# Layer 0's linear attention in chunks of 64 tokens in place of 128

## The chip, the cores and the metric

One core of one Trainium2 chip. The metric is the device time of one launch in microseconds (us), as the median of several runs. The kernel before took 1550.02 us in the median of six runs (1547.88 to 1553.77).

## What is computed

Two transformer layers over x of shape 16 x 512 x 128 (batches, tokens, width) in fp32. Each layer normalises x and adds an attention and a feed-forward part to it. Layer 0 has a linear attention with 16 heads of 8, and a mixture of 8 experts (top 2) with a shared expert. Layer 1 has a softmax attention in chunks of 64 queries with a gate on each head's sum, and a channel mix. The change touches layer 0's attention alone:

```python
def step(carry, qkv):                      # over the tokens; q, k after rope and elu(x) + 1
    K_sum, KV = carry
    q_t, k_t, v_t = qkv
    K_sum = K_sum + k_t
    KV = KV + k_t[..., :, None] * v_t[..., None, :]
    num = jnp.einsum('bhd,bhde->bhe', q_t, KV)
    den = jnp.maximum(jnp.einsum('bhd,bhd->bh', q_t, K_sum), EPS)
    return ((K_sum, KV), num / den[..., None])
```

Nothing forces a step for each token: within a chunk of tokens the kernel takes scores q k^T, masks them causally and multiplies by v; all earlier chunks come in as one product of q with the running state, the sum of k v^T over them. A column of ones beside v gives the denominator.

## The kernel before

**Four chains of work.** The 16 batches go in four groups of four. For each group there are four Python generators: `dispatch` (normalise, route, and scatter the rows to their experts' slots by an indirect DMA), `slot_tiles` (the experts on 39 slots of 128 rows at the most), `layer0` (linear attention and shared expert, `first_layer` per batch) and `layer1` (`head`, `body`, `tail` per batch). Every `yield` of a generator ends a step. A loop at the end of `two_layers` gives each chain a start and a time per step, from `PACE`, `LAYER_STEPS` (steps per batch) and `LAYER_US`, and always advances the chain that is due first. That settles the rank of each operation.

**A planner.** No instruction is issued there. `Program.call` records each operation with an estimated cost, what it reads and writes, and `Program.run` simulates the five engines on these costs and emits, engine by engine, the operation of the lowest rank that is ready and whose buffers are free. So the order on each engine is the planner's, and its costs only shape that order. Operations in a `with program.unit()` are emitted together. Scatters and fetches by indirect DMA on POOL (`send`, line 1202, and `fetch`, line 1221) are kept `SPACE` ns apart on the planner's clock, and each is made to wait for the PE operation that had passed by then. Since all operations are emitted from one helper, nearly all have line 323 in the profile; line 328 is the same helper where a full matmul is emitted as four of 32 output columns each (`strips`), which the planner does when the matmul before it was not of the full form, since TensorE then needn't change its tiling.

**Layer 0's attention, per batch.** `linear_operands` makes q, k and v for four tiles of 128 tokens, applies rope and elu + 1, copies v into `vpads` (strips of 32 columns: 16 of v, two of ones, the rest belongs to the neighbour) and `vstrips`, and then the running states: for t = 0, 1, 2 a matmul of k^T with v of tile t is added into one bank of PSUM, and after each VectorE (DVE) copies the sum so far, masked by `blocks`, to `states[t]`. It transposes q and k (`qT`, `kT`), and makes four copies of `qT` with all but one of four heads' rows zeroed (`q0m`). `linear_attention` then goes through the four tiles: `scores(t)` is a unit of eight matmuls with 32 rows each (row group j of `kT` against two copies of q, 256 columns, the four j into four banks), and DVE multiplies the 4 x 512 scores by the causal mask into two `am`; `weigh(t)` is a unit on one bank with 8 matmuls of the state with q (128 rows, 32 output columns, 128 tokens; none for t = 0) and 16 of the strips of v with `am`; ScalarE (ACT) copies the result. Every second tile `finish` transposes, divides by the denominators and writes `o0n`. The first two batches run side by side, the second on buffers that layer 1 doesn't need yet (`LENT`). PSUM has eight banks, handed out by the planner, in ones or pairs.

Of the kernel before, what the change touches and what calls it, by code (L numbers as in the profile page):

```python
# [29 lines left out]
F32 = mybir.dt.float32  # L30
# [3 lines left out]
ALU = mybir.AluOpType  # L34
AX = mybir.AxisListType

P = 128
# [17 lines left out]
def slot_count(gt):  # L55
# [13 lines left out]
HALVES = 2 * NT  # L69

VPAD = (H - 1) * (PAIR + 2) + 32

# [15 lines left out]
    ("ident", P), ("cos", NT * 4), ("sin", NT * 4), ("blocks", 8 * (PAIR + 2)), ("pick", 4),  # L88
    ("causal", P), ("rank", E), ("upper", P), ("ones", P), ("tile", SLOT_TILES),
    ("aug_q", 2 * HALVES), ("aug_k", 4 * HALVES), ("own", 2), ("parity", 4),  # L90
# [16 lines left out]

LAYER_STEPS = (16, 40)

# [144 lines left out]
class Op:  # L254


    def __init__(self, engine, emit, cost, later, index):
        self.engine, self.emit, self.cost, self.later, self.index = engine, emit, cost, later, index
        self.needs, self.bases, self.wrote, self.then = set(), set(), set(), []
        self.missing, self.ready, self.result, self.done = 0, 0.0, None, False  # L260

        self.spaced = False

        self.form, self.strips, self.narrow = None, None, False

# [11 lines left out]

TURN = {(32, 128): 208, (128, 32): 138, (128, 128): 148}

SPACE = 1900  # L280

PACE = (
    (0.1, 0.4, 0.26, 0.8, 0.0, 0.8, 0.0, 1.23),
    (0.3, 0.4, 0.2, 0.8, -0.09, 1.0, 0.22, 1.0),
    (0.0, 0.58, 0.27, 0.76, 0.18, 1.0, 0.0, 1.0),
)


class Program:
# [21 lines left out]
    def call(self, name, api, method, args, kw):  # L311
# [18 lines left out]
        if name == "PE":  # L330
            later = 60.0
            form = (args[1].shape[0], o.shape[0])
            if method == "transpose":
                cost = 112.0
            elif args[1].shape[0] == 32:
                cost = max(0.425 * n, 56.0)
            elif o.shape[0] == 32:
                cost = max(0.425 * n, 56.0)
            else:
                cost = max(1.68 * n, 224.0)  # L340
# [16 lines left out]
        if name == "PE":  # L357
            (self.unit_of[0] if self.unit_of else op).form = form
            op.strips = strips if method == "matmul" and form == (P, P) else None
# [46 lines left out]
    def run(self):  # L406
# [20 lines left out]
        while emitted < len(self.ops):  # L427
# [27 lines left out]
            if op.spaced:  # L455
                self.spaced_to = start + SPACE
                while len(self.passed) > 1 and self.passed[1][0] <= start:
                    self.passed.pop(0)
                op.paced = self.passed[0][1] if self.passed else None
            end = start + op.cost  # L460
            if name == "PE":
                if self.form != (P, P) and all(part.strips for part in op.parts or [op]):
                    op.form, op.narrow = (P, 32), True
                if op.form != self.form:
                    end += TURN.get(op.form, 148)
                    self.form = op.form
            if name == "PE":
# [135 lines left out]
def two_layers(ctx: ExitStack, tc: tile.TileContext, x, small, const, w_fc, w_proj, out):  # L603
# [144 lines left out]
    states = []  # L748
    for i in range(NT - 1):
        st = fixed.tile([P, 8, 32], F32, tag=f"state{i}", name=f"state{i}")  # L750
        G.memset(st, 0.0)
        states.append(st)
# [156 lines left out]
    def tokens_to_heads(o, name, tag):  # L909
# [10 lines left out]
    OWN = {  # L920
        "vpad": 0, "qr": ("qr", 1), "T": ("q0T", "k0T", 1), "q0m": ("q0m", 2), "am": ("am", 2),
        "oTs": "oTs0", "o": "o0n", "oT": "oT_a0", "xs": ("xs", 1),
    }
    LENT = {
        "vpad": 2, "qr": ("ka", 2), "T": ("qa", "qa", 2), "q0m": ("probs", 4), "am": ("ka", 2),
        "oTs": "oTs1", "o": "o1n", "oT": "oT_a1", "xs": ("rr", 2),
    }
    OWN["vstrips"], OWN["states"] = vstrips, states

    def lent_layer():  # L930

        a = p3.tile([P, 1024], F32, tag="probs", name="vstrips_lent", bufs=4)
        LENT["vstrips"] = a[:, 0 : NT * 8 * (PAIR + 2)].rearrange(
            "p (t s e) -> p t s e", t=NT, e=PAIR + 2
        )
        G.memset(a, 1.0)
        a = p3.tile([P, 1024], F32, tag="probs", name="states_lent", bufs=4)
        LENT["states"] = [
            a[:, i * 256 : (i + 1) * 256].rearrange("p (s e) -> p s e", e=32) for i in range(NT - 1)
        ]  # L940
        G.memset(a, 0.0)

    def linear_operands(xnT, b, home):
# [50 lines left out]

        pst = one(f"state_{b}")
        for t in range(NT - 1):
            M.matmul(
                pst[:, 0 : 8 * (PAIR + 2)], qr[:, t, D : 2 * D],
                vs[:, t, :, :].rearrange("p s e -> p (s e)"),
                start=(t == 0), stop=(t == NT - 2), skip_group_check=True,  # L1000
            )
            V.tensor_tensor(
                states[t][:, :, 0 : PAIR + 2],
                pst[:, 0 : 8 * (PAIR + 2)].rearrange("p (s e) -> p s e", e=PAIR + 2), blocks,
                ALU.mult,
            )
        yield
# [3 lines left out]
        for s, (tag, n) in enumerate(((q_tag, "q0T"), (k_tag, "k0T"))):  # L1011
# [7 lines left out]
            both.append(oT)  # L1019
        qT, kT = both  # L1020
        qms = []
        for u in range(2):
            tag, bufs = home["q0m"]
            qm = (p3 if tag == "probs" else p2).tile(
                [P, 2, T], F32, tag=tag, name=f"q0m_{b}_{u}", bufs=bufs
            )
            for o in range(2):
                r = 2 * u + o
                S.activation(qm[:, o, :], qT, AF.Copy, scale=c_("pick")[:, r : r + 1])
            qms.append(qm)  # L1030
        yield
        return qT, kT, qms

    def linear_attention(operands, b, home):
# [3 lines left out]

        def scores(t):

            scs = [big(f"sc0_{b}_{t}_{pr}") for pr in range(2)]
            cols = slice(t * P, (t + 1) * P)
            with program.unit():
                for u in range(2):
                    for j in range(4):
                        rows = slice(32 * j, 32 * j + 32)
                        M.matmul(
                            scs[j // 2][:, j % 2, 2 * u * P : 2 * (u + 1) * P].rearrange(
                                "p (o q) -> p o q", o=2
                            ),  # L1050
                            kT[rows, cols], qms[u][rows, :, cols], start=True, stop=True,
                        )
            ams = []
            for pr, sc in enumerate(scs):
                tag, bufs = home["am"]
                am = p2.tile([P, 2, 512], F32, tag=tag, name=f"am_{b}_{t}_{pr}", bufs=bufs)
                V.tensor_tensor(
                    am.rearrange("p j (t q) -> p j t q", q=P),
                    sc.rearrange("p j (t q) -> p j t q", q=P),
                    causal.unsqueeze(1).unsqueeze(1).to_broadcast([P, 2, NT, P]), ALU.mult,  # L1060
                )
                ams.append(am)
            return ams

        def weigh(t, ams, oT):

            po = one(f"o0_{b}_{t}")

            with program.unit():
                for u in range(2):  # L1070
                    for j in range(4):
                        o = po[32 * j : 32 * j + 32, u * P : (u + 1) * P]
                        if t:
                            M.matmul(
                                o, states[t - 1][:, 4 * u + j, :], qT[:, t * P : (t + 1) * P],
                                start=u == 0, stop=False, skip_group_check=True,
                            )
                    for o_ in range(2):
                        c = (2 * u + o_) * P
                        for j in range(4):  # L1080
                            M.matmul(
                                po[32 * j : 32 * j + 32, u * P : (u + 1) * P],
                                strip(vp, t, 8 * u + 2 * j + o_), ams[j // 2][:, j % 2, c : c + P],
                                start=t == 0 and u == 0 and o_ == 0, stop=(o_ == 1),
                                skip_group_check=True,
                            )
            S.copy(oT[:, (t % 2) * 2 * P : (t % 2 + 1) * 2 * P], po[:, 0 : 2 * P])

# [15 lines left out]

        for t in range(NT):
            if t % 2 == 0:
                oT = p2.tile([P, T], F32, tag=home["oTs"], name=f"oTs0_{b}_{t // 2}")
            ams = scores(t)
            yield
            weigh(t, ams, oT)  # L1110
            yield
            if t % 2:
                finish(oT, t // 2)
                yield
        return tokens_to_heads(o, f"a0_{b}", home["oT"])
# [82 lines left out]
    def send(rows, slot, row, clear, sent):  # L1198
# [14 lines left out]
        i.bases.add(rows.base)  # L1213
        i.spaced = True
        after(i, [clear])
        sent.append(i)

    def fetch(o, results, slot):
# [6 lines left out]
        )  # L1225
        i.spaced = True

# [514 lines left out]
def _constants():  # L1742
# [6 lines left out]
    i = np.arange(P)  # L1749
    c["causal"] = (i[None, :] >= i[:, None]).astype(f)  # L1750
    e = np.arange(PAIR + 2)
# [84 lines left out]
```

## Time and profile before

| | |
|---|---|
| median of six runs | 1550.02 us (1547.88 to 1553.77) |
| the profiled execution | 1542.83 us, span in the profile 1541.1 us |
| mean granted clock of TensorE | 0.985 |
| instructions | 53614, of them 23070 matmul and 23070 weight-load records on TensorE |
| am, the mask on the scores (DVE) | 128 x 1219 ns, 151.0 us busy |
| states (DVE) | 48 x 303 ns, 14.5 us busy |
| matmul records of the scores, of the states with q, of v with am | 1024, 768, 2048 |

In the profile PE is TensorE's matmuls and PEld its weight loads, DVE VectorE, ACT ScalarE, POOL GpSimd. Groups are named by what they write and read: `banks<-q0m,k0T` are the scores, `banks<-am,vpad` and `banks<-q0T,state` the two parts of weigh, `banks<-vstrips,qr` the states' matmuls; `banks<-qa,ka` and `banks<-ka,qa` are layer 1's scores, of which `maxima` takes maxima and `ex` the exponential. A form such as 32\*128 stands for the rows and output columns of TensorE that a matmul uses. A matmul of fp32 is recorded twice. Records of matmuls that run side by side overlap, and their ends are modelled, so the starts are what can be relied on.

### The profile page before, as it was taken

How to read it: one execution, taken by the hardware profiler on the slowest of the kernel's cores; microseconds unless marked ns; L12 is line 12 of the kernel's file. 1: busy time of each engine (PE TensorE's matmuls, PEld its weight loads, DVE VectorE, ACT ScalarE, POOL GpSimd, SP SyncE). 2: the span in 40 equal slices, each digit the busy share in tenths (PEclk: the TensorE clock that was granted, in tenths of full speed). 3: DMA queues.
4: the chain of work that ended last, by engine and by line, in shares of the span. 5: the costliest groups of instructions: out<-in, count | busy, mean ns of one | idle time of the engine just before them, and what ended most of it. 6: DMA issues, size and time to landing. Idle time of an engine off the chain costs nothing.

```text
span 1541.1 us, 53614 instructions
## 1 busy us (share of the span) xinstructions
PE 1409.4 (91%) x23070; PEld 927.0 (60%) x23070; DVE 1067.0 (69%) x2289; ACT 864.1 (56%) x1369; POOL 390.8 (25%) x425
## 2 busy tenths in 40 slices
PE   4788989899999999999999999999999989887876
PEld 2577877666666657666666666665766545533433
DVE  7874432787877776687684868586858896865673
ACT  3335565565665655656656656755665545455434
POOL 3540142432036241215300240200001512442310
PEclk9899999999999999999999999999999999999998
DMA  6247777655254545243432434322411100000000
GB/s 195 91 151 206 214 237 206 184 164 156 75 161 138 155 142 149 74 136 118 132 93 61 126 115 128 109 85 65 126 47 46 43 21 20 17 15 8 8 1 14
DMA packets 150237, 163.08 MB, mean 106 GB/s; under 512 B 12912, under 2 KB 97648, under 8 KB 150000
## 3 DMA queue, kind: packets, MB, share of 16 engines
q1 hardware_dynamic: 141808, 142.86, 31.2%
q0 software_dynamic: 8192, 16.79, 3.4%
q8 instruction: 181, 2.97, 0.8%
q14 instruction: 56, 0.46, 0.1%
HBM read 118.71 MB, written 40.89 MB: 104 GB/s over the span
## 4 chain that ended last, share of the span: by engine, by line
PE 77%; DVE 11%; ACT 7%; issue 3%; DMA 1%; SPq 0%; POOL 0%; DVEq 0%; ACTq 0%
PE banks L323 56%; PE banks L328 21%; DVE maxima L323 5%; ACT ex L323 3%; ACT hg L323 2%; DVE am L323 1%; DVE by_cos L323 1%; ACT q0m L323 1%; DMA back<-results,pl_slot 1%; DVE by_sin L323 0%; ACT vpad L323 0%; ACT h L323 0%; DMA raw_wqkv<-in_small 0%; ACT vstrips L323 0%; DVE gf_z L323 0%
## 5 line engine op out<-in xcount | busy, mean ns | idle before, releaser
L323 DVE TENSOR_REDUCE maxima<-banks 128x2 f32<-128x768 f32 (+2 forms) x448 | 385.7, 914 | 75.6 <-PE banks L323 73.9
L323 ACT ACTIVATE ex<-banks 128x1024 f32<-128x1024 f32 x320 | 311.4, 1021 | 133.0 <-PE banks L323 127.8
L323 DVE TENSOR_TENSOR am<-banks,const_sb 128x1024 f32<-128x1024 f32 x128 | 151.0, 1219 | 108.8 <-PE banks L323 100.5
L323 PE MATMUL banks<-ka,qa 32*128 32x512 f32 (+2 forms) x1792 | 184.9, 505 | 29.5 <-ACT ex L323 18.6
L323 PE MATMUL banks<-qa,ka 32*128 32x512 f32 (+3 forms) x2048 | 192.5, 462 | 18.9 <-DVE maxima L323 11.7
L1221 POOL DMA_INDIRECT back<-results,pl_slot x128 | 127.3, 995 | 290.1 <-PE banks L323 192.9
L1202 POOL DMA_INDIRECT rows<-xn,pl_slot x128 | 127.1, 993 | 290.1 <-DVE pl_slot L323 172.9
L323 PE MATMUL banks<-ex,vpad 128*32 128x512 f32 (+3 forms) x2048 | 174.3, 443 | 2.2 <-issue 1.0
L323 PEld LDWEIGHTS banks<-qa,ka 32*128 32x128 f32 x2048 | 94.7, 185 | 94.6 <-DVE maxima L323 24.3
L323 ACT ACTIVATE hg<-banks 128x512 f32<-128x512 f32 x156 | 93.2, 598 | 99.7 <-PE banks L328 77.7
L323 PEld LDWEIGHTS banks<-ka,qa 32*128 32x128 f32 x1792 | 80.2, 185 | 93.5 <-ACT ex L323 28.7
L328 PE MATMUL banks<-xgT,wf 128*32 128x128 f32 x3296 | 109.2, 274 | 3.7 <-ACT ex L323 1.4
L323 PEld LDWEIGHTS banks<-ex,vpad 128*32 128x32 f32 x2048 | 53.3, 109 | 93.2 <-issue 63.5
L328 PE MATMUL banks<-wp,hg 128*32 128x128 f32 x3200 | 100.0, 276 | 9.6 <-ACT hg L323 4.8
L328 PEld LDWEIGHTS banks<-xgT,wf 128*32 128x32 f32 x3296 | 89.2, 110 | 29.7 <-issue 9.0
L328 PEld LDWEIGHTS banks<-wp,hg 128*32 128x32 f32 x3200 | 88.1, 111 | 28.0 <-ACT hg L323 9.5
L323 ACT COPY oTs<-banks 128x256 f32<-128x256 f32 (+1 forms) x96 | 42.8, 446 | 88.0 <-PE banks L323 84.6
L323 ACT ACTIVATE hg<-hg 128x1024 f32<-128x1024 f32 x80 | 82.9, 1037 | 2.5
L323 PE MATMUL banks<-am,vpad 128*32 128x128 f32 x2048 | 78.2, 273 | 2.6 <-DVE am L323 2.1
L323 PE MATMUL banks<-q0m,k0T 32*128 32x256 f32 x1024 | 73.3, 399 | 2.2 <-DVE am L323 0.9
L323 ACT COPY yg<-banks 128x256 f32<-128x256 f32 x80 | 29.4, 367 | 68.6 <-PE banks L328 51.6
L323 PEld LDWEIGHTS banks<-am,vpad 128*32 128x32 f32 x2048 | 58.0, 110 | 11.0 <-DVE am L323 3.1
(224 smaller groups left out, 2224.2 us busy)
## 6 DMA issues: line engine op xcount, KB each, us to landing
wf<-in_w_fc SPq DMA_DIRECT2D x156, 256.0 KB
wp<-in_w_proj SPq DMA_DIRECT2D x156, 256.0 KB
rows<-zeros SPq DMA_DIRECT2D x4, 2496.0 KB
results<-yg SPq DMA_DIRECT2D x76, 128.0 KB
xg<-rows SPq DMA_DIRECT2D x36, 256.0 KB
x_in<-in_x SPq DMA_DIRECT2D x16, 256.0 KB
x<-x SPq DMA_DIRECT2D x16, 256.0 KB
out<-rr SPq DMA_DIRECT2D x16, 256.0 KB
```

The source lines that it names most:

```text
L323: return getattr(api, method)(*map(made, args), **{k: made(a) for k, a in kw.items()})
L328: yield api.matmul(to[at : at + 32], weights[:, at : at + 32], *rest, **kw)
L1202: i = nc.gpsimd.indirect_dma_start(out=rows.made()[:, :], out_offset=bass.IndirectOffsetOnAxis(ap=slot.made(), axis=0), in_=row.made(), in ...
L1221: "POOL", lambda: nc.gpsimd.indirect_dma_start(out=o.made(), out_offset=None, in_=results.made()[:, :], in_offset=bass.IndirectOffsetOnAxi ...
```

## The change

A chunk is now 64 tokens (`CH`), eight in a batch (`CHUNKS`). Scores and weigh go over pairs of tiles, `tp`, in place of single tiles. A chunk's keys are rows of one half of the partitions: the scores of the chunk c = 0 of a tile go to partitions 0 to 63, those of c = 1 to 64 to 127, so the two bank pairs that held one tile's scores hold two tiles', and one causal mask of 64 columns serves both. Seven states are needed in place of three: seven matmuls of 64 rows in one unit, into three banks; DVE masks the first six in one instruction and the seventh in another, and adds them up in place with six additions. Weigh takes a pair of banks, one for each c; the states' matmuls have 32 rows and 32 columns now (row group j and strip j), those of v with `am` 64 rows and 32 columns. The four copies of q are one tile for the batches that use their own buffers. The planner's costs and turns get the new forms, `LAYER_STEPS`, `PACE` and the spacing of indirect DMAs other values. Beside that, the weight loads and DMAs are the same.

```diff
-LAYER_STEPS = (16, 40)
+LAYER_STEPS = (12, 40)
...
-SPACE = 1900
+SPACE = 1500
+SPACE_FIRST = 1500
 PACE = (
-    (0.1, 0.4, 0.26, 0.8, 0.0, 0.8, 0.0, 1.23),
-    (0.3, 0.4, 0.2, 0.8, -0.09, 1.0, 0.22, 1.0),
-    (0.0, 0.58, 0.27, 0.76, 0.18, 1.0, 0.0, 1.0),
+    (0.1, 0.4, 0.31, 0.8, 0.0, 0.8, 0.01, 1.28),
+    (0.3, 0.41, 0.12, 0.8, -0.26, 1.0, 0.25, 1.0),
+    (-0.27, 0.45, 0.41, 0.67, 0.05, 1.0, 0.21, 0.54),
 )
...
-        pst = one(f"state_{b}")
-        for t in range(NT - 1):
-            M.matmul(
-                pst[:, 0 : 8 * (PAIR + 2)], qr[:, t, D : 2 * D],
-                vs[:, t, :, :].rearrange("p s e -> p (s e)"),
-                start=(t == 0), stop=(t == NT - 2), skip_group_check=True,
-            )
-            V.tensor_tensor(
-                states[t][:, :, 0 : PAIR + 2],
-                pst[:, 0 : 8 * (PAIR + 2)].rearrange("p (s e) -> p s e", e=PAIR + 2), blocks,
-                ALU.mult,
-            )
+        n = 8 * (PAIR + 2)
+        pst, last = big(f"state_{b}"), one(f"state_last_{b}")
+        with program.unit():
+            for i in range(CHUNKS - 1):
+                t, c = i // 2, i % 2
+                rows = slice(c * CH, (c + 1) * CH)
+                M.matmul(
+                    pst[:, c, t * n : (t + 1) * n] if i < CHUNKS - 2 else last[:, 0:n],
+                    qr[rows, t, D : 2 * D], vs[rows, t, :, :].rearrange("p s e -> p (s e)"),
+                    start=True, stop=True, skip_group_check=True,
+                )
+        V.tensor_tensor(
+            states[0][:, :, 0:n].rearrange("p (t c) e -> p c t e", c=2),
+            pst[:, :, 0 : 3 * n].rearrange("p c (t e) -> p c t e", t=3),
+            c_("blocks").unsqueeze(1).unsqueeze(1).to_broadcast([P, 2, 3, n]), ALU.mult,
+        )
+        V.tensor_tensor(states[1][:, 0, 0:n], last[:, 0:n], c_("blocks"), ALU.mult)
+        for i in range(1, CHUNKS - 1):
+            upto = state_of(states, i)[:, 0:n]
+            V.tensor_tensor(upto, upto, state_of(states, i - 1)[:, 0:n], ALU.add)
...
+        def scores(tp):
+            scs = [big(f"sc0_{b}_{tp}_{pr}") for pr in range(2)]
             with program.unit():
+                for r, n, qm in qms:                      # own buffers: one r, n = 4
+                    for t, c, half, cols in parts(tp):    # two tiles, two chunks
+                        at = (t % 2) * 4 * CH + r * CH
+                        for j in range(4):
+                            rows = slice(32 * j, 32 * j + 32)
+                            M.matmul(
+                                scs[j // 2][half, j % 2, at : at + n * CH].rearrange(
+                                    "p (o q) -> p o q", q=CH
+                                ),
+                                kT[rows, cols], qm[rows, :, cols], start=True, stop=True,
+                            )
...
+        def weigh(tp, ams, oT):
+            po, begun = big(f"o0_{b}_{tp}"), set()
...
             with program.unit():
+                for t, c, _, cols in parts(tp):
+                    for u in range(2):
                         for j in range(4):
+                            if 2 * t + c:
+                                o, kw = to(t, c, u, j)    # strip j of bank c, 64 columns
+                                at = (4 * u + j) * (PAIR + 2)
+                                rows = slice(32 * j, 32 * j + 32)
+                                M.matmul(
+                                    o, state_of(states, 2 * t + c - 1)[rows, at : at + 32],
+                                    qT[rows, cols], stop=False, **kw,
+                                )
+                for t in (2 * tp, 2 * tp + 1):
+                    for u in range(2):
+                        for o_ in range(2):
+                            for j in range(4):
+                                for c in range(2):
+                                    half = slice(c * CH, (c + 1) * CH)
+                                    o, kw = to(t, c, u, j)
+                                    at = (t % 2) * 4 * CH + (2 * u + o_) * CH
+                                    M.matmul(
+                                        o, strip(vp, t, 8 * u + 2 * j + o_)[half, :],
+                                        ams[j // 2][half, j % 2, at : at + CH],
+                                        stop=(o_ == 1), **kw,
+                                    )
...
-        for t in range(NT):
...
+        for tp in range(NT // 2):
+            oT = p2.tile([P, T], F32, tag=home["oTs"], name=f"oTs0_{b}_{tp}")
+            ams = scores(tp)
+            yield
+            weigh(tp, ams, oT)
+            yield
+            finish(oT, tp)
+            yield
```

## Prediction

> **What bounds the kernel now.** I read the page first: its busy line for TensorE (PE), and the chain that ended last.
>
> ```profile
> span 1541.1 us, 53614 instructions
> ...
> PE 1409.4 (91%) x23070; PEld 927.0 (60%) x23070; DVE 1067.0 (69%) x2289; ACT 864.1 (56%) x1369; POOL 390.8 (25%) x425
> ...
> PE 77%; DVE 11%; ACT 7%; issue 3%; DMA 1%; SPq 0%; POOL 0%; DVEq 0%; ACTq 0%
> ```
>
> PE carries 77% of the chain, DVE 11%. But a share is an average, so I read next the windows of 100 us (columns: length, then busy time of PE, PEld, DVE, ACT, POOL).
>
> ```profile
> 0.00:100.00 100.00, 69.56 (x760) 50.05 (x761) 78.39 (x246) 34.21 (x72) 46.67 (x68) 0.91 0.42 129
> ...
> 400.00:500.00 100.00, 99.52 (x1764) 68.95 (x1766) 79.42 (x197) 62.33 (x102) 35.31 (x38) 1.00 0.43 128
> ...
> 1400.00:1541.10 141.10, 105.05 (x1184) 50.77 (x1176) 76.23 (x152) 65.09 (x84) 28.08 (x20) 0.92 0.03 9
> ```
>
> Three stages. The first 100 us leave PE 30 us idle and DVE is the fullest. From 300 to 1200 PE idles only some 20 of 900 us: there the end moves by what PE saves. The last 241 us (84.94 of 100 us busy, then 105.05 of 141.10) are layer 1 nearly alone, with 51 us of PE idle. The windows of the tile q0m place layer 0's scores: 176 of 1024 matmul records before 115.6 us and none after 1298. So 2.75 of 16 batches run in the first stage and 13.25 where PE binds or nearly.
>
> The durations of overlapping matmuls mean little, so I price by the timeline of PE, from the start of one group to the start of the next (start, length, engine, line, operands, count). Every fp32 matmul is two records: the 16 matmuls of a weigh unit on am stand as 32.
>
> ```profile
> 624.23 0.44 PE L328 MATMUL banks<-small_sb,xnT 128*32 128x8 f32 x32
> 624.51 1.08 PE L328 MATMUL banks<-xgT,wf 128*32 128x128 f32 x32
> ...
> 711.09 1.15 PE L323 MATMUL banks<-q0m,k0T 32*128 32x256 f32 x16
> 712.16 1.08 PE L328 MATMUL banks<-xgT,wf 128*32 128x128 f32 x32
> ...
> 716.04 0.43 PE L323 MATMUL banks<-q0T,state 128*32 128x128 f32 x8
> 716.29 0.62 PE L323 MATMUL banks<-am,vpad 128*32 128x128 f32 x16
> 716.72 0.40 PE L323 MATMUL banks<-q0T,state 128*32 128x128 f32 x8
> 716.94 0.62 PE L323 MATMUL banks<-am,vpad 128*32 128x128 f32 x16
> 717.49 0.66 PE L323 MATMUL banks<-const_sb,o1n 128*128 128x128 f32 x4
> ...
> 749.64 1.06 PE L328 MATMUL banks<-wpj_s,h 128*32 128x128 f32 x32
> 750.52 0.40 PE L328 MATMUL banks<-small_sb,oT_a 128*32 128x128 f32 x8
> 751.61 0.43 PE L328 MATMUL banks<-vstrips,qr 128*32 128x144 f32 x8
> 751.97 1.14 PE L323 MATMUL banks<-ka,qa 32*128 32x512 f32 x8
> ```
>
> A scores unit takes 712.16 - 711.09 = 1.07 us, a weigh unit with state 717.49 - 716.04 = 1.45 (without, at t = 0, 507.66 - 506.65 = 1.01), a state matmul 0.36. Sixteen matmuls of 128 columns on four column tiles, with the same form after them, take 750.52 - 749.64 = 0.88 us, 55 ns each; the 1.01 holds a change of form of 0.13. At 8 columns they take 624.51 - 624.23 = 0.28 us, 17.5 ns each: the floor this trace shows for one fp32 matmul with its weight load.
>
> **The change part by part**, per batch, PE first. Before: 4 x 1.07 + 1.01 + 3 x 1.45 + 3 x 0.36 = 4.28 + 5.36 + 1.08 = 10.72 us.
>
> *Scores.* Two units in place of four, each of 16 matmuls of 256 columns on eight tiles (four row groups by two halves of the output). If the halves run side by side, each tile has two matmuls, as each row group has now: 2 x 1.07 = 2.14. If only four tiles run at a time, 2 x (1.72 + 0.21) = 3.86, the 0.21 being what 1.07 holds over 4 x 256 columns at the 55 ns rate (0.86). No row has eight tiles. I take 2.14: four row groups together (q0m) and four column tiles with different moving data together (wpj_s) both have rows. [...]
>
> *Weigh, states.* 24 matmuls of 128 columns become 56 of 64 (seven chunks, two units, four strips), on the four diagonal tiles. Bounds per matmul: 17.5 ns (the 8-column row) and 55 (nothing gained from halving): 0.98 to 3.08 us. I take half of 55, 27.5, since 128 columns are far over the floor: 1.54.
>
> *Weigh, own chunk.* 64 matmuls of 128 columns become 128 of 64, with 64 rows each, on eight tiles. If eight overlap, the floor of 17.5 ns binds: 2.24 us; if four, 27.5: 3.52; by a straight line between the 8- and the 128-column rows, 35: 4.48. I take 22, midway between the first two: 2.82. Each of the two units now enters two forms, so changes stay at four: 0.52. Weigh: 1.54 + 2.82 + 0.52 = 4.88 against 5.36.
>
> *States.* Seven matmuls of 64 rows and 144 columns, in one unit. Full-array rows go one at a time at 224 ns per 128 columns (xgT,wf 128x128, cadence 112 a record), 252 for 144: 1.76 alone, or four deep in two row halves 1.01, with 0.15 of form change 1.16 to 1.91. I take 1.16, as row groups do overlap in q0m's row. The three rounds in which DVE had to read one bank before PE went on are gone; the waits view has 1.3 us for them in all, so nothing.
>
> After: 2.14 + 4.88 + 1.16 = 8.18, so PE gives back 2.54 us a batch, 40.6 in all.
>
> *DVE.* The mask on am falls from 128 to 64 instructions of 1219 ns: -78.0 us. The states' 48 of 303 ns (-14.5) become, per batch, one of 864 elements (between 690 ns at 512 and 1219 at 1024: 1.05), one of 0.30 and six adds of 144 elements (224 ns at 64, 291 at 128: 0.30), 3.15 x 16 = +50.4. Net -42 us. In the PE-bound stage that is worth nothing: DVE is at 75 to 80%. Behind the adds on DVE's queue stand layer 1's reductions of maxima, for which PE waited 21.3 us in all; a run of eight is 2 us longer than what stood there, but twice a batch two am of 2.4 us are gone from the same queue. The first weigh waits for the adds; transposes, four q0m on ACT (722 ns each) and the first am lie before it and cover them. Without that cover it would be 3 us a batch on one chain with three others to fill PE.
>
> *ACT*: 64 copies of 375 ns become 32 of 586, -5 us, off the path. *Banks*: scores hold four banks twice a batch, not four times; weigh takes two for half as many units; the states take three at once. Nothing either way.
>
> *POOL's spacing* falls from 1900 to 1500 in the planner's clock. The first 32 scatters run from 47.0 to 105.5 us, 1.83 each; 32 x 0.4 is up to 12.8 us earlier for the first slot tiles, which wait for all of them. From 100 to 140 PE idles 8.6 us, but the DMA share is 0.7 to 0.9 until 260. Bounds -9 to +5 (scatters that crowd the weights' loads); I take 0. *PACE* and LAYER_STEPS change only the order: the idle in the first and last stages, 30 + 51 us, may move by some 10 either way; I take 0.
>
> The sum: 13.25 batches x 2.54 = 33.7 us come off where PE binds. In the first stage 2.75 batches x 2.6 us of DVE = 7; half of it, 3.5, since scatters and DMA run beside. What is late next: with less of layer 0 to fill in, PE's waits on ex (24.4 us in all) and maxima (21.3) grow; a tenth of the gain, 3.5. Net -34. The profiled execution took 1542.8 us (its span 1541.1 and 1.7 around it) and would take 1509; the median of the six runs, 1550.0, lies 7.2 above it, so **1516 us**.
>
> **The rivals.** *Half of it comes back as waiting*: layer 1 alone keeps PE at 79% (190 of 241 us), 97% with fillers. If the smaller layer 0 lets one more batch of layer 1 (60 us) run alone, 60 x 0.18 = 11 us, and with worse order at the start some 17: 1533. For it: the last stage; against it: mid-run a batch of layer 1 takes 86 us, not 60, so PE is what holds it.
>
> *Better*: own-chunk matmuls at the 17.5 ns floor (0.58 a batch, 9 us) and the scatters' 9 us: 1498. For it: the idle from 100 to 140.
>
> *The tiles don't overlap (it does not do what it says)*: scores 3.86, weigh 1.54 + 3.52 + 0.52 = 5.58, states 1.91: 11.35, +0.63 x 13.25 = +8, less 3 at the start: 1555.
>
> *The other side: the states' diagonal tiles take turns.* The 56 matmuls have four row groups that write four strips of the same bank at once; in every row of the trace four row groups (q0m, qa, ka) write four banks. One at a time, a matmul of 64 columns costs half of 224 ns, 112, so 6.27 in place of 1.54: +4.73 x 13.25 = +63, and 1516 + 63 = 1579. It decides from a price of 73 ns each on, where the 34 us are gone (2.54 a batch over 56 is 45 ns above 27.5). Against it: the strips are different partitions, and column tiles of one bank do overlap in wpj_s's row. [...]
>
> **How the numbers follow.** Forecast 0.62 (1502 to 1532, from the prices of 17.5 to 35 ns and the order); half comes back 0.13; better 0.08; no overlap 0.11; turns 0.06. Faster: 0.62 + 0.13 + 0.08, less 0.02 for their upper ends, 0.81; no overlap straddles zero, 0.04 of it within 0.2%; slower 0.15. (0.2%, 3 us, is about what a measurement of this kernel can tell from no change.) The range leaves out the turns and part of the better case and takes in no overlap: 1495 to 1556.
>
> **What would show it.** The scores' form has 64 output columns, and 32 records start to start take about 1.1 us, not 1.9. A weigh unit of two tiles takes about 2.4 us, of it 0.7 to 0.9 for the states; over 4 us means turns. DVE falls to about 1025 us, PE to about 1370, and PE stays at 97% or more from 300 to 1200. If PE's busy time falls by 35 us or more and the span by less than 20, waiting has taken the place; if the span falls by over 50, the start or the order gave it.

## The result

The changed kernel takes 1558.8 us in the median of 20 runs (1550.51 to 1568.76), the kernel before 1550.18 (45 runs): ratio 1.0054, 95% interval 1.0041 to 1.0066. It is 0.5% slower; 1516 us was predicted. The profiled execution took 1564.1 us.

The profile's page after, in three lines: the span, the engines' busy time, and the DMA queue that the page marks as instruction (packets, MB, share).

```profile
span 1562.3 us, 57575 instructions
...
PE 1401.3 (90%) x25080; PEld 917.1 (59%) x25080; DVE 1029.2 (66%) x2305; ACT 856.1 (55%) x1337; POOL 389.4 (25%) x424
...
q8 instruction: 196, 3.21, 0.9%
```

DVE fell by 38 us, as forecast. PE fell by 8, not by 40, though it has more matmul records (25080 against 23070). The mean granted clock is 0.966 (0.985 before). Two windows that answer to those shown of before:

```profile
0.00:100.00 100.00, 60.40 (x1106) 40.89 (x1107) 67.62 (x229) 29.66 (x60) 42.90 (x62) 0.85 0.41 124
400.00:500.00 100.00, 96.31 (x2052) 66.52 (x2052) 76.57 (x207) 58.87 (x96) 33.37 (x36) 0.98 0.44 131
```

PE is idler at the start (60 of 100 us in place of 70, clock 0.85 in place of 0.91) and in the middle too (96.3 in place of 99.5). What it waits for is in the waits view of PE (releaser: us in total, times, longest); the first and the last line are of a kind that summed to 5.2 us before.

```profile
PE banks L331 <- issue: 31.5, 25, 3.3
PE banks L331 <- ACT ex L331: 27.4, 43, 1.2
PE banks L331 <- DVE maxima L331: 21.1, 30, 1.4
...
PE banks L336 <- issue: 4.1, 2, 2.2
```

The two lines of that kind before:

```profile
PE banks L328 <- issue: 4.2, 4, 2.2
PE banks L323 <- issue: 1.0, 1, 1.0
```

"Issue" is time for which the profile shows no semaphore. It grew by 30 us; ex and maxima hardly moved (24.4 and 21.3 before). Thirteen of the 27 waits, 20.3 us, fall before layer 1's first `ex`, which starts at 338 us (at 313 before). Where they happen is in PE's timeline:

```profile
657.04 0.87 PE L331 MATMUL banks<-q0T,state 32*32 32x64 f32 x48
657.85 1.45 PE L331 MATMUL banks<-am,vpad 64*32 64x64 f32 x124
661.49 0.30 PE L331 MATMUL banks<-am,vpad 64*32 64x64 f32 x4 [2.19 <-issue]
661.72 1.08 PE L336 MATMUL banks<-xgT,wf 128*32 128x128 f32 x32
...
730.89 0.87 PE L331 MATMUL banks<-q0T,state 32*32 32x64 f32 x48
731.70 1.48 PE L331 MATMUL banks<-am,vpad 64*32 64x64 f32 x128
733.11 0.66 PE L331 MATMUL banks<-const_sb,oTs 128*128 128x128 f32 x4
```

The same unit, twice. At 731.70 the own-chunk group of 64 matmuls takes 733.11 - 731.70 = 1.41 us to the next group. At 657.85 PE stops after 124 of 128 records, in the middle of a unit in which nothing is waited for, and the group takes 3.87. Of the 32 own-chunk groups ten take 1.41 us; the others take 1.76 to 4.82, and all together 79.7: 34.6 us more than 32 x 1.41. Of these, 28.5 lie inside the groups; the other 6 are mostly two waits behind a group, one on issue (2.24 us) and one on a DMA (3.34).

Each matmul of fp32 is two matmul and two weight-load records, four instructions (in bursts, below, 400 matmuls are 800 and 800 records). That makes 2 x 25080 / 196 = 256 instructions for each packet of q8, and 3.21 MB / 196 = 16 KB a packet. So the first theory, FETCH in the later expectations: PE uses up its instructions faster than they come. The trace's records of q8 bear it out in place: each of the 27 times that PE goes on after a wait on issue lies 2.3 to 2.9 us after a packet of q8 began, though a packet begins only every 8 us in the mean. And of TensorE's instructions ahead of each of the 27, in order of start, 193 or 194 are left over from full blocks of 256. The rivals: FORM (tiles of 64 and 32 rows overlap badly or read as idle to the clock) and ORDER (the new `PACE` and spacing are a worse order). The first expectations have ORDER against "code", which is FETCH and FORM in one.

### The profile page after: what moved, and what is told of

It is laid out like the page before. It is cut to its first block, busy times and chain, and to the rows that moved or that the text cites. A ratio compares the mean times of both kernels' runs of the same rounds, so it can differ in the third digit from the quotient of the medians.

```text
span 1562.3 us, 57575 instructions
## 1 busy us (share of the span) xinstructions
PE 1401.3 (90%) x25080; PEld 917.1 (59%) x25080; DVE 1029.2 (66%) x2305; ACT 856.1 (55%) x1337; POOL 389.4 (25%) x424
## 3 DMA queue, kind: packets, MB, share of 16 engines
q8 instruction: 196, 3.21, 0.9%
## 4 chain that ended last, share of the span: by engine, by line
PE 42%; DVE 7%; ACT 5%; issue 2%; DMA 1%; POOL 0%; DVEq 0%; ACTq 0%; POOLq 0%
PE banks L331 31%; PE banks L336 11%; DVE maxima L331 4%; ACT ex L331 4%; DMA back<-results,pl_slot 0%; DVE rr L331 0%; DVE by_cos L331 0%; DMA out<-rr 0%; DMA x<-x 0%; DVE am L331 0%; DVE by_sin L331 0%; DVE gf_z L331 0%; ACT q0m L331 0%; DVE state L331 0%; POOL xn L331 0%
## 5 line engine op out<-in xcount | busy, mean ns | idle before, releaser
L331 PE MATMUL banks<-ka,qa 32*128 32x512 f32 (+2 forms) x1792 | 194.2, 519 | 25.9 <-ACT ex L331 18.2
L331 PE MATMUL banks<-ex,vpad 128*32 128x512 f32 (+3 forms) x2048 | 178.7, 451 | 3.1 <-DVE maxima L331 1.8
L331 DVE TENSOR_TENSOR am<-banks,const_sb 128x1024 f32<-128x1024 f32 x64 | 75.5, 1219 | 47.5 <-PE banks L331 47.3
L331 ACT COPY oTs<-banks 128x512 f32<-128x512 f32 x64 | 37.5, 585 | 110.5 <-PE banks L331 110.3
L336 PE MATMUL banks<-wp,hg 128*32 128x128 f32 x2592 | 81.6, 278 | 7.7 <-DMA results<-yg 3.3
L331 POOL TENSOR_TENSOR rr<-rr,x 128x512 f32<-128x512 f32 x16 | 20.5, 1279 | 269.3 <-DVE rr L331 269.2
L336 PEld LDWEIGHTS banks<-wp,hg 128*32 128x32 f32 x2592 | 72.2, 112 | 19.8 <-issue 10.5
L331 PE MATMUL banks<-wp,hg 128*128 128x128 f32 x600 | 74.2, 276 | 0.9 <-ACT hg L331 0.8
L331 PEld LDWEIGHTS banks<-wp,hg 128*128 128x128 f32 x600 | 70.6, 192 | 6.3 <-ACT hg L331 3.8
L331 PE MATMUL banks<-am,vpad 64*32 64x64 f32 x4096 | 54.7, 225 | 21.5 <-issue 21.3
```

The costliest lines, as they stand in the source:

```text
L331: return getattr(api, method)(*map(made, args), **{k: made(a) for k, a in kw.items()})
L336: yield api.matmul(to[at : at + 32], weights[:, at : at + 32], *rest, **kw)
```

## The experiments

Ratios are to the kernel before, measured beside each run. "Issue" is the sum of PE's waits on it and "clock" the mean granted clock, both in the profiled execution.

| run | ratio (95% interval) | median, us | issue, us | clock |
|---|---|---|---|---|
| before | 1 | 1550.2 | 5.2 | 0.985 |
| after | 1.0054 (1.0041, 1.0066) | 1558.8 | 35.6 | 0.966 |
| code_old_order | 1.0302 (1.0280, 1.0323) | 1598.4 | 42.7 | 0.960 |
| before_new_order | 1.0035 (1.0018, 1.0052) | 1559.2 | 6.4 | 0.972 |
| old_pace | 1.0291 (1.0274, 1.0309) | 1596.5 | 37.7 | 0.961 |
| old_space | 1.0034 (1.0015, 1.0052) | 1558.0 | 35.6 | 0.971 |
| wide128 | 0.9835 (0.9818, 0.9852) | 1523.4 | 4.4 | 0.975 |
| wide64 | 0.9774 (0.9759, 0.9789) | 1515.4 | 9.7 | 0.970 |
| before_split | 1.0214 (1.0201, 1.0227) | 1582.4 | 12.4 | 0.977 |
| per_tile | 1.0104 (1.0084, 1.0125) | 1564.0 | 34.8 | 0.975 |
| heads_in_halves | 0.9839 (0.9808, 0.9870) | 1522.8 | 13.6 | 0.980 |
| before_split_same_order | 1.0131 (1.0101, 1.0161) | 1569.4 | 13.9 | 0.982 |
| wide64_old_pace | 0.9988 (0.9968, 1.0008) | 1549.1 | 8.5 | 0.961 |

### Is it the order? (code_old_order, before_new_order, old_pace, old_space)

The new code with the old `PACE` and spacing; the old code with the new `PACE` and a spacing of 1500; the new code with one of the two old at a time.

```diff
-PACE = ((0.1, 0.4, 0.31, 0.8, 0.0, 0.8, 0.01, 1.28), ...)    # old_pace, code_old_order
+PACE = ((0.1, 0.4, 0.26, 0.8, 0.0, 0.8, 0.0, 1.23), ...)
-SPACE = 1500                                                 # old_space, code_old_order
+SPACE = 1900
```

> The changed attention with PACE and both spacings of the kernel before (1900); LAYER_STEPS stays at 12, since a batch has 12 steps now. Theory order: the code gives back the 1.38 us a batch that the timeline of after shows on PE (10.72 before; 2.10 + 6.06 + 1.18 after), some 18 us where PE binds, and the new PACE and spacing lose 25 by starting layer 1 late; then this run takes about 1532 us, 0.988 of before, and the first ex starts at 305 to 313 us as before. Theory code: the new forms themselves cost it (weigh units with 14 ns a record, and a clock halved 109 us in all in place of 48); then it takes 1553 to 1562 as after does, and the granted clock is 0.966 to 0.974 again.

> The kernel before with PACE of after and a spacing of 1500. Theory order: 25 us slower than before, 1575 us (1.016), with the first ex some 25 us late. Theory code: within 0.3% of before, and a granted clock of 0.985.

> After with PACE of before; the spacings stay at 1500. Theory order with PACE as its cause: as in the run of the changed code with the old PACE and spacing, about 1532 us. With the spacing as its cause: 1555 to 1560. Theory code: 1553 to 1562.

> After with both spacings at 1900 and its own PACE. Theory order with PACE as its cause: 1555 to 1560 us, as after. With the spacing as its cause (scatters that crowd the loads of weights): about 1535. Theory code: 1553 to 1562.

The spacing is worth nothing (1.0034 against 1.0054, intervals that overlap). `PACE` is worth much, but the other way: with the old one the new code takes 1596.5 us, 38 more, outside the ranges of both theories. On the old code the new `PACE` and spacing cost 0.35%. So the loss isn't the new order; the issue waits are there in either.

### Fewer instructions for the same part (wide128, wide64)

The own-chunk part goes out as 32 matmuls of 128 columns, on all 128 rows (wide128) or on 64 (wide64). Both leave out separations that the result needs (their expectations say which), so they price the instructions and replace nothing. The order on every engine stays.

```diff
-for u in range(2):
-    for o_ in range(2):
-        for j in range(4):
-            for c in range(2):
-                M.matmul(o, strip(vp, t, 8 * u + 2 * j + o_)[half, :], ams[j // 2][half, j % 2, at : at + CH], ...)
+for u in range(2):
+    for j in range(4):
+        for c in range(2):
+            M.matmul(                                # wide128: without [half]
+                po[32 * j : 32 * j + 32, c, 2 * (t % 2) * CH : 2 * (t % 2) * CH + 2 * CH],
+                strip(vp, t, 8 * u + 2 * j)[half, :], ams[j // 2][half, j % 2, at : at + 2 * CH], ...)
```

> The changed kernel, but the own-chunk part of a weigh unit is issued as 32 matmuls of 128 columns on all 128 rows in place of 64 matmuls of 64 columns on 64 rows: half the PE instructions, as many columns times rows or more. (It leaves out the separation of the two chunks and of two heads of a pair: their sums are added. Order on every engine as in the changed kernel.) By the rows, 32 such matmuls take 32 x 55 ns = 1.76 us, 0.35 to 0.5 us a unit MORE than the 1.27 to 1.41 us that an unstalled own-chunk group takes: 32 units, +11 to +16 us of array work. Theory FETCH (PE runs out of instructions because the small matmuls use up 256 instructions in under 2 us): PE's waits on 'issue' fall from 35.6 us to under 12, halvings of the clock become fewer, mean clock 0.975 or more, and in spite of more array work the time falls: 1535 to 1552, ratio 0.990 to 1.001. Theory FORM (the small tiles themselves overlap badly or read as idle to the clock): no help is needed from fewer instructions; array work is added, 1565 to 1575. Theory ORDER (the new order of the engines' work is worse): as the changed kernel, 1555 to 1565, with fewer issue waits but as much idle.

> The changed kernel, but the own-chunk part is issued as 32 matmuls of 128 columns and 64 rows (form 64*32) in place of 64 of 64 columns: half the instructions in the same form of tile. (It leaves out the separation of two heads of a pair. Order as in the changed kernel.) If eight tiles overlap, 32 x 27.5 ns = 0.88 us a unit against 1.41; if only four, 1.76. Theory FETCH: 'issue' waits of PE under 12 us (35.6 in the changed kernel), own-chunk groups of 64 records 0.9 to 1.3 us and none over 2, time 1520 to 1540, ratio 0.980 to 0.993. Theory FORM: issue waits fall less than half, clock stays near 0.966, time 1548 to 1562. Theory ORDER: 1550 to 1562, fewer issue waits but the gain turned into idle on ex or banks.

wide128 does more array work, 1.95 us a group in most places where 1.41 would do:

```profile
558.61 2.02 PE L331 MATMUL banks<-am,vpad 128*32 128x128 f32 x64
560.56 1.14 PE L331 MATMUL banks<-qa,ka 32*128 32x512 f32 x8
```

Yet it is 35 us faster than the changed kernel. It has half the own-chunk instructions, but also another form and more columns in a matmul; wide64 keeps the form 64\*32, and heads_in_halves, below, the 64 columns. wide64 takes 1515.4 us. Both are faster than the ranges given for FETCH. The waits on issue of wide64:

```profile
PE banks L336 <- issue: 5.9, 4, 2.7
PE banks L331 <- issue: 3.8, 5, 1.3
```

And its timeline at the place that stalled above (the same groups in the same order):

```profile
628.70 0.87 PE L331 MATMUL banks<-q0T,state 32*32 32x64 f32 x48
629.51 1.16 PE L331 MATMUL banks<-am,vpad 64*32 64x128 f32 x64
630.59 1.08 PE L336 MATMUL banks<-xgT,wf 128*32 128x128 f32 x32
```

1.08 us in place of 3.87, in the form 64*32, next to 32*32: FORM falls. Of the 43 us between the changed kernel and wide64, 32 x (1.41 - 1.09) = 10 are array time. The other 33 went with the instructions: PE's waits on issue fell by 25.9 us, and what the own-chunk groups take over their array time by 27.2 (34.6 to 7.4). The two overlap, and the rest of the 33 wasn't traced; the clock can hold 8 of it at most by estimate, half of the difference between the 108 us for which it was at half in the changed kernel and the 92 in wide64.

### More instructions in the kernel before (before_split, before_split_same_order)

Every weigh matmul of 128 columns becomes two of 64.

```diff
-M.matmul(po[32 * j : 32 * j + 32, u * P : (u + 1) * P], strip(...), ams[j // 2][:, j % 2, c : c + P], ...)
+for q in (0, 64):
+    M.matmul(po[32 * j : 32 * j + 32, u * P + q : u * P + q + 64], strip(...),
+             ams[j // 2][:, j % 2, c + q : c + q + 64], ...)
```

> The kernel before, but every matmul of a weigh unit on 128 columns is two on 64 columns: the same sums, form, and order on every engine; 16 to 24 matmuls of a unit become 32 to 48, so 128 to 192 instructions where there were 64 to 96. Array time is the same if a matmul of 64 columns takes half of 55 ns. Theory FETCH: the before kernel's 5.2 us of 'issue' waits rise to 12 to 30, clock falls below 0.98, time +8 to +30 us, ratio 1.005 to 1.020; in this kernel other dense groups on the same instructions stand beside. Theory FORM or ORDER: forms and order are unchanged, so within 0.3%: ratio 0.998 to 1.003.

> before_split again, with the planner told the old price of a weigh unit, so that the order on all five engines is that of the kernel before, instruction for instruction but for the doubled matmuls (in before_split the planner had the price 3% lower, and the order was another). Theory FETCH: of the 33 us that before_split lost, 15 to 30 stay: array time of 12 us more (the groups' starts in before_split: own chunk 65.7 to 74.8 us, states 21.1 to 23.8) plus stalls: ratio 1.009 to 1.020, issue waits over 10 us. Rival (the 33 us were the other order): only the array's 5 to 12 us stay, ratio 1.002 to 1.008, issue waits 5 us as in the kernel before.

Of before_split's 2.1% a part was order: the planner had been given a slightly other price. With the order of the kernel before, 1.3% stay, 20 us (16 to 25). Its waits on issue:

```profile
PE banks L328 <- issue: 9.5, 11, 2.0
PE banks L323 <- issue: 4.4, 4, 2.3
```

These are 8.7 us more than before; the groups on `am` and on the states take 10.7 us more from start to start (65.7 to 74.0 and 21.1 to 23.5), a part of which is waits on issue within them. So twice as many matmuls cost time in the old code as well, some 9 of the 20 us as waits on issue.

### Units of half the size (per_tile)

```diff
-weigh(tp, ams, oT)
+weigh(2 * tp, ams, oT)
+yield
+weigh(2 * tp + 1, ams, oT)
```

(`LAYER_STEPS` rises from 12 to 14 with it.)

> The changed kernel, but weigh is one unit for each tile of 128 tokens (40 to 48 matmuls, 160 to 192 instructions) with its own pair of banks, in place of one unit for two tiles (88 to 96 matmuls, 352 to 384 instructions), so that layer 1's matmuls, with more array time per instruction, can be put between. 16 * 2 more copies of 256 columns on ACT, two more changes of form a batch (+0.3 us each), the planner's order is another. Theory FETCH: 'issue' waits of PE fall from 35.6 to under 15 us, clock 0.975 or more, time 1525 to 1548, ratio 0.983 to 0.998. Theory FORM: 1560 to 1575 (more changes of form, same tiles). Theory ORDER: anything from 1540 to 1600 and issue waits don't matter to it.

A miss: the issue waits stay at 34.8 us. One place in the timeline:

```profile
1086.13 0.43 PE L331 MATMUL banks<-q0T,state 32*32 32x64 f32 x16
1086.49 0.86 PE L331 MATMUL banks<-am,vpad 64*32 64x64 f32 x64
1087.28 0.66 PE L331 MATMUL banks<-const_sb,xg 128*128 128x128 f32 x4
1087.87 0.65 PE L331 MATMUL banks<-q0T,state 32*32 32x64 f32 x32
1088.44 0.84 PE L331 MATMUL banks<-am,vpad 64*32 64x64 f32 x63
1091.51 0.24 PE L331 MATMUL banks<-am,vpad 64*32 64x64 f32 x1 [2.22 <-issue]
```

Here the planner puts the two halves 1.7 us apart, with 0.6 us of other work between, so the same 352 instructions go out in some 3 us at PE's own pace. From the first half's own-chunk group to the second's it is 1.4 us at the least and 3.4 in the median of the 32 units; in 26 of them it is less than the 5.3 us in which 352 instructions come by the next experiment. Split in two, the units saved nothing here (34.8 us of issue waits against 35.6), as their parts stayed together.

### The supply by itself (bursts)

```diff
+for k, (rows, n) in enumerate(((128, 128), (128, 96), (128, 64), (64, 64), (128, 8))):
+    for m in range(400):
+        M.matmul(pp[32 * j : 32 * j + 32, c, 0:n], probe[half, 0, 0:32], probe[half, 0, 128 : 128 + n], ...)
```

> The kernel before, with five bursts of 400 matmuls (1600 PE instructions) after all of its work, each after 12 us or more without PE work: 128 columns, 96, 64, then 64 columns with 64 rows on eight tiles, then 8 columns; all else 128 rows, four column tiles. The total time is of no interest. Theory FETCH: without a limit they would take 400 x 55 = 22 us, 41 ns = 16.5, 27.5 ns = 11, 20 ns = 8, 17.5 ns = 7 us. If PE's instructions come in blocks of 256 (64 matmuls) and a block takes some 2 us to come, the first bursts run at their own pace, and from 64 columns on each settles at the same pace, about 2 us or more for 64 matmuls (31 ns or more each), with gaps at every 64th: the last three bursts all take 12 us or more. Rival (no limit on the stream): the last three take 11, 8 and 7 us with no gap.

PE's timeline of the second, third and fourth burst (96 columns, 64, and 64 with 64 rows):

```profile
1585.25 10.73 PE L323 MATMUL banks<-probe 128*32 128x96 f32 x427 [8.36 <-DVE probe L323]
1596.61 2.84 PE L323 MATMUL banks<-probe 128*32 128x96 f32 x128 [0.63 <-issue]
1600.37 2.84 PE L323 MATMUL banks<-probe 128*32 128x96 f32 x128 [0.91 <-issue]
...
1615.17 5.66 PE L323 MATMUL banks<-probe 128*32 128x64 f32 x267 [8.38 <-DVE probe L323]
1622.29 1.99 PE L323 MATMUL banks<-probe 128*32 128x64 f32 x128 [1.46 <-issue]
1625.76 1.99 PE L323 MATMUL banks<-probe 128*32 128x64 f32 x128 [1.48 <-issue]
1629.78 1.99 PE L323 MATMUL banks<-probe 128*32 128x64 f32 x128 [2.03 <-issue]
...
1646.51 3.38 PE L323 MATMUL banks<-probe 64*32 64x64 f32 x235 [8.44 <-DVE probe L323]
1651.47 1.47 PE L323 MATMUL banks<-probe 64*32 64x64 f32 x128 [1.58 <-issue]
1655.21 1.67 PE L323 MATMUL banks<-probe 64*32 64x64 f32 x128 [2.28 <-issue]
1658.96 2.04 PE L323 MATMUL banks<-probe 64*32 64x64 f32 x128 [2.07 <-issue]
```

Four of the five bursts run freely for a while and then stop after every 128 records, which is 64 matmuls or 256 instructions. From one restart to the next it takes 3.76, 3.47, 4.02, 3.74, 3.75 us, and 3.9 at 8 columns: in all four forms 256 instructions in about 3.8 us, 67 per us or 59 ns a matmul. From one burst's first stop to the next burst's it is 640, 768 and 768 records, multiples of 128: the stops stand at fixed places of the instruction stream, as the 27 of the changed kernel do. The last three bursts ran freely for 267, 235 and 203 records first, 400 to 530 instructions; FETCH takes these for what had come ahead (the stock) and what came meanwhile, and no view shows a stock itself. The burst of 128 columns took 24 us for 400, 60 ns a matmul, without a wait, at a granted clock of 0.90; by estimate that is 24 x 0.90 / 400 = 54 ns at the full clock. So the matmul of 128 columns on four column tiles, of which the kernel before is full, runs at just about the pace of the supply (54 to 60 ns against 59). In the kernel before, most blocks of 256 cost no wait: five waits, 5.2 us in all, for 181 packets. In the last three bursts every block costs 1.4 to 2.3 us.

With this the units can be put side by side:

| unit | PE instructions | us | per us |
|---|---|---|---|
| before: scores, one tile | 32 | 1.07 | 30 |
| before: weigh, one tile | 96 | 1.45 | 66 |
| after: scores, two tiles | 64 | 1.05 | 61 |
| after: weigh, states | 96 to 128 | 0.80 to 1.03 | 120 to 124 |
| after: weigh, own chunk | 256 | 1.41 | 182 |
| the supply, in bursts | 256 | 3.8 | 67 |

A batch of layer 0 had 492 PE instructions in 10.7 us of array time (46 per us); now it has 892 in 7.9, or 13.2 us of supply. So by these rates the own chunk of a weigh unit needs a stock to run at its own pace (1.41 us against 3.8 for as many instructions). The own-chunk groups without a stop had 307 instructions in the 8 us before them, in the mean, the others 390; the two overlap widely, so the neighbours alone don't decide it.

### The whole computation with fewer instructions (heads_in_halves)

The two partition halves of `am` hold the two heads of a pair for one chunk, in place of two chunks of one head; k is copied with each head's rows zeroed, v is made a second time so that each half has the chunk's tokens.

```diff
-kT[rows, cols], qm[rows, :, cols]                             # 64 keys; four heads' q: 16 of 256 columns
+km[rows, i * P : (i + 1) * P], qu[rows, :, cols]              # 2 heads x 64 keys; u = 0, 1: 16 of 128
...
-M.matmul(o, strip(vp, t, 8 * u + 2 * j + o_)[half, :], ams[j // 2][half, j % 2, at : at + CH], ...)   # 64
+M.matmul(o, pair(vp, 2 * t + c, 4 * u + j), ams[j // 2][:, j % 2, at : at + CH], ...)                 # 32
...
+for i in range(CHUNKS):
+    for o in range(2):
+        M.matmul(pv[o * CH : (o + 1) * CH, i * CH : (i + 1) * CH], xnT[:, i * CH : (i + 1) * CH],
+                 wqkv0[:, 2, :].rearrange(...)[:, :, o, :], ...)      # the values of head o of each pair
```

> A version of the changed kernel with the whole computation: in the scores the two partition halves hold the two heads of a pair, for one chunk, in place of the two chunks of one head. Then one own-chunk matmul takes both heads (128 rows, 64 columns): 32 of them in a weigh unit in place of 64, as in wide64. The values must lie in both halves for that: 16 more matmuls of 64 columns a batch (form 128*64) and other copies on ACT. Terms against the changed kernel, per batch: own chunk 2 x (1.09 - 1.41) = -0.64 us; the 16 matmuls at 56 ns (half of 112 for 64 columns on the full array) and a change of form, +1.0: together +0.4, +5 us in the 13 batches where PE binds. The planner's order is another (+-8 us). Theory FETCH: the stalls of 35 us and the halvings that follow them go: 1518 to 1540, ratio 0.980 to 0.994, 'issue' waits under 12 us. Theory ORDER or FORM: 1558 to 1575.

1522.8 us, 1.6% under the kernel before (1.3 to 1.9%), within the range given; the waits on issue, 13.6 us, are a little over the 12 named. These waits, then the own-chunk group of a weigh unit in PE's timeline:

```profile
PE banks L336 <- issue: 10.5, 10, 2.2
PE banks L331 <- issue: 3.1, 6, 1.2
```

```profile
655.13 1.10 PE L331 MATMUL banks<-am,vpad 128*32 128x64 f32 x64
656.16 1.14 PE L331 MATMUL banks<-qa,ka 32*128 32x512 f32 x8
```

32 matmuls of 64 columns do in 1.03 us here (0.92 to 2.48 in all units) what 64 did in 1.41 to 4.82.

### What is left of the order (wide64_old_pace)

> wide64 (own chunk as 32 matmuls of 128 columns and 64 rows; it leaves out the separation of two heads of a pair) with the PACE of the kernel before; the order on all engines is that of old_pace, which took 1596.5 us with 37.7 us of issue waits. Question: are the 38 us that PACE is worth on the new code apart from the stalls, or does the new PACE only spread the same stalls better? If apart: as much comes off as from the changed kernel to wide64 (-43 us, ratio -0.028): 1550 to 1558, ratio 1.000 to 1.005, and 38 us stay between the two PACEs. If PACE only works against the stalls: 1515 to 1530, ratio 0.978 to 0.988. In both cases issue waits under 12 us.

"Apart", though 1549.1 us lies 1 us under its range. With most of the stalls gone the new code on the old `PACE` is as fast as the kernel before, and 34 us stay between the two. From the first `ex` of layer 1 to the last it takes 1209 us with the old `PACE`, as in the kernel before (1208), and 1178 in wide64. In PE's timeline, pauses of over 0.5 us between starts sum to 392 us, against 373 in wide64 and 351 before: 19 of the 34 us. Which places in the order they come from wasn't traced.

## Why the prediction was wrong

**The array's prices were right.** Scores 1.05 us for two tiles (1.07 taken), states' part 0.80 and 1.03, own chunk 1.41 twice: weigh 4.65 us a batch (4.88 taken); the states' matmuls 1.18 (1.16). That is 7.9 us in place of 10.7: 2.8 a batch (2.54 taken). "No overlap" and "the tiles take turns" fall with it: the states' records start 14 to 17 ns apart in the mean, with four row groups in one bank (48 in the one group, at 74.8 us, with a wait on issue in it); one at a time they would be some 56 apart (half of the 112 a record that the prediction read for 128 columns). Weigh units over 4 us were named as the sign of turns; they occur, but in all but that one the states' part is as short as elsewhere.

**DVE and the rest were right**: DVE 1029 us (about 1025 forecast), the seven states 1059 ns and 308 for each addition (1.05 and 0.30 taken), the spacing nothing.

**The step that failed is the one from array time to PE's time.** "PE gives back 2.54 us a batch" counted what the array does with a matmul, and nothing for bringing its instructions. The change goes from 123 matmuls a batch to 223. PE's busy time fell by 8 us in place of 40, its waits on issue rose from 5.2 to 35.6, and the missing term is worth 33 us in the time, by wide64. 1516 + 33 = 1549; the changed kernel took 1558.8, so some 10 us stay open. That wide64 comes to 1515.4, next to the forecast, is luck in part: its own chunk is cheaper by 0.64 us a batch than the forecast had it, and by the same sum it should have come to some 1508. The rival "half of it comes back as waiting" had waiting in it, but put it in layer 1's alone stage, on ex and maxima, which stayed where they were.

**The 17.5 ns floor was no floor for a row of matmuls.** It came from groups of 16 matmuls, 64 instructions, where the last three bursts ran freely for 400 to 530. After that the bursts say 59 ns, to the end of a row of 400. The page of before had the hint, 181 packets for 2 x 23070 instructions, beside rows at 55 ns, which use up 256 instructions in 3.5 us:

```profile
q8 instruction: 181, 2.97, 0.8%
```

**`PACE` was taken at 0, within 10 us, and is worth 34 to 38 on the new code** (5 to its harm on the old). So two terms were off in opposite ways: with the old `PACE` the array's gain wouldn't have reached the end even without stalls (1549.1). That 13.25 batches pass all of their saving on was not a property of the stage alone: it needs an order made for it.

**The clock** went down with it, 0.985 to 0.966; that wasn't forecast. It was at half for 108 us in place of 48, which can cost 30 us at most by estimate (half of the difference), and it isn't separated from the stalls here. It can't be the main cause: wide64 has 0.970 and is 43 us faster, with an even lower clock in the first 100 us (0.80, against 0.85).

## What to carry to other kernels

Before cutting matmuls into smaller ones, count instructions as well as columns: an fp32 matmul is four, and in bursts a row of small ones (8 to 64 columns) went freely for 100 to 135 matmuls after a pause of 8 us, then at 59 ns each, at 8 columns as at 64. Compare each unit's instructions per us with the supply (67 in bursts) and look what runs next to it; the units of 352 to 384 instructions in 2.2 to 2.4 us mostly stall here (22 of 32 own-chunk groups take 1.76 us or more in place of 1.41), though the kernel's mean is 32 per us. Where a finer form saves array time, look for the arrangement that keeps the number of matmuls, as the two heads in the halves did, and price an order's parameters by a run with the old ones.

## What the runs showed of the hardware

- Where PE outran its instructions in the bursts, it stopped after every 256 of them, one block in 3.8 us in the mean (3.47 to 4.02). In the changed kernel the packets of q8 that began 2.3 to 2.9 us before the 27 waits ended lasted 0.9 to 1.5 us. If those of the bursts did too, most of the 3.8 us is not the transfer; what it is stays open. The clock isn't it: with 0.92 granted the restarts are 3.47 to 4.02 us apart (64 columns), with 0.50 it is 3.74 to 4.02 (8 columns).
- The stalls alone don't account for the granted clock. The bursts of 128 columns, of 64 columns, of 64 columns with 64 rows, and of 8 columns (length, PE busy, PEld busy, three idle engines, clock, DMA share and rate): the second stalls at every block and is granted 0.92, more than the first, which never stalls (0.90); the last two, with PE busy for 55% of the time in place of 61, are granted 0.67 and 0.50. What lowers it isn't shown.

```profile
1552.60:1576.60 24.00, 24.00 (x796) 23.64 (x800) 0.00 (x0) 0.00 (x0) 0.00 (x0) 0.90 0.05 15
...
1615.20:1637.90 22.70, 13.95 (x800) 13.18 (x800) 0.00 (x0) 0.00 (x0) 0.00 (x0) 0.92 0.02 4
...
1646.50:1666.90 20.40, 11.32 (x798) 10.34 (x800) 0.00 (x0) 0.00 (x0) 0.00 (x0) 0.67 0.02 4
1675.70:1696.80 21.10, 11.64 (x800) 11.18 (x800) 0.00 (x0) 0.00 (x0) 0.00 (x0) 0.50 0.01 4
```

- Where nothing stops it, a matmul of 64 columns and 64 rows on eight tiles takes 20 to 22 ns in the changed kernel (64 of them 1.27 us from the first start to the last, 1.41 to the next group), one of 128 columns on the same tiles 34 in wide64 (32 of them 1.08 us to the next group).
